# Upper two levels of a table lookup: masks on ScalarE as borders of the index, in place of bits on VectorE

## The chip, the cores and the metric

The kernel runs on one core of one Trainium2 chip. The metric is the device time of one execution in microseconds (us). Engines are named as the profile names them: PE is TensorE (matmul), PEld its weight loads, DVE is VectorE, ACT is ScalarE, POOL is GpSimd, SP is SyncE, which issues most DMAs. Each engine works through its own queue in order; an instruction that waits holds up all that stands behind it on that engine.

## The reference

Input x is 8 x 1024 x 512 (float32). What is computed, cut to what matters:

```
xn = layernorm(x)
q  = xn @ Wq ; gate = softmax(xn @ Wg)                       # 3 gates
blended = sum_i gate_i * (((q @ k_i.T) * decay_i**dist * causal) @ v_i)
s  = blended @ Wo * out_scale
w  = lut[idx]         # for gate_idx, up_idx (1376 x 512), down_idx (512 x 1376); lut has 16 floats
h  = silu(xn @ w_gate.T) * (xn @ w_up.T) ; f = h @ w_down.T
out = x + s * silu(f)
```

The change lies in `w = lut[idx]`: each index is an integer from 0 to 15, and each weight is one of 16 table values.

## The kernel before, in words

The work has two phases. Phase 1 (about the first 588 us of the profile) goes over the eight batches of x: layernorm statistics, transposes, projections to values and features, and the recurrent part chunk by chunk. Beside it, it turns the indices into float weights and writes those, with sums of their blocks, to DRAM. Phase 2 is the feed-forward part and the output: large products on PE with PSUM banks copied and added by ACT and DVE.

In phase 1 everything is written as generators that are advanced in turn; `keep_order` then fixes the order in which the code was traced, on PE, DVE, ACT and POOL. An iteration of the loop at L762 (one chunk of 128 rows, some 9.5 us) has this order:

1. `project` of the newer batch: transposes on PE (`pt` L452), copy to SBUF by ACT (`xnT` L453), normalizing and statistics by ACT (L446, L447, L436, L437), with POOL for the power (L438, L439);
2. `chunks` of the older batch: transposes `pk` (L670) on PE, three scaled copies by ACT (`ks` L673);
3. one step of the weight builder (L778), steps of the features (L520 on PE, with copies by ACT at L533 to L558 and sums by DVE at L530 to L555), one or two builder steps (L785);
4. `chunks`: scores `psc` (L677) on PE, DVE multiplies them (`pr` L679) and prepares the next queries (`ga` L652), POOL `qb` (L656);
5. three or four builder steps (L787), a step of the features;
6. `project`: values `pv` (L459) on PE, copy by ACT (`v` L462); `chunks`: `pu` (L687) and `po` (L701) on PE, copies by ACT (`bl` L702, `R` L708, `pu` L715).

The PSUM tiles pt, pk, psc, pv, po rotate through three banks (`p_c`). So the next pk takes the bank of pv, and can't start until ACT has copied v (L462); the next psc takes that of po.

The builder (`ffn_weights`) runs through 16 lookups: eleven for gate and up (128 partitions x 1024 indices, the last 768), one for the tail of down (96 x 512) and four for down (1024). A seventeenth (`left_weights`, 1024) lies in phase 2, at 603 to 666 us. They are numbered 1 to 17 here. Index tiles are loaded by SP one lookup ahead (two buffers).

A lookup (`look_up`, L215) is a binary tree. Three instructions on DVE (L220) take bits 1, 2 and 3 of the index as byte masks; one (L223) turns the index in place into a word that is all ones where bit 0 is set. Eight leaves (L227) give one of two table values each by bit 0, and seven predicated copies (L244) choose between neighbours: bit 1 at level 1, bit 2 at level 2, bit 3 at level 3. The three bits, L223, each leaf and each copy are one builder step each, 19 in all. The mask tiles have one buffer each, so a mask of one lookup can't be written until the last copy of the lookup before that reads it is done.

Of the kernel before, what the change touches and what calls it, by code (L numbers as in the profile page):

```python
# [9 lines left out]
F32 = mybir.dt.float32  # L10
BF16 = mybir.dt.bfloat16
I32 = mybir.dt.int32
U8 = mybir.dt.uint8
AF = mybir.ActivationFunctionType
ALU = mybir.AluOpType
AX = mybir.AxisListType

P = 128
# [30 lines left out]
def recurrent_block(ctx: ExitStack, tc, x, wq, wk, wv, wo, wg, decay_logits, out_scale, lut, gidx, uidx, didx, out):  # L49
# [19 lines left out]
    nc = tc.nc  # L69
# [16 lines left out]
    const = ctx.enter_context(tc.tile_pool(name="const", bufs=1))  # L86
# [62 lines left out]
    make_identity(nc, ident)  # L149
    nhalf = const.tile([P, 1], F32)  # L150
    nc.gpsimd.memset(nhalf, -0.5)


    dl = const.tile([P, NI], F32)
# [59 lines left out]

    def look_up(build, dst, iv, rows, n):  # L215

        bits = [build.tile([P, n], U8, name=f"bit{j}", tag=f"bit{j}") for j in (1, 2, 3)]
        low = iv.bitcast(U8).rearrange("p (n four) -> p n four", four=4)[:, :, 0]
        for j in (1, 2, 3):
            nc.vector.tensor_scalar(bits[j - 1][:rows, :n], low, 1 << j, None, ALU.bitwise_and)  # L220
            yield

        nc.vector.tensor_scalar(iv, iv, 31, 31, ALU.logical_shift_left, ALU.arith_shift_right)  # L223
        yield

        def leaf(o, k):
            nc.vector.tensor_scalar(  # L227
                o.bitcast(I32),
                iv,
                lut_x[:rows, k, :],  # L230
                lut_i[:rows, k, 0:1],
                ALU.bitwise_and,
                ALU.bitwise_xor,
            )

        def tree(o, level, k):
            if level == 0:
                leaf(o, k)
                yield
                return  # L240
            t = build.tile([P, n], F32, name=f"leaf{level}", tag=f"leaf{level}")
            yield from tree(o, level - 1, k)
            yield from tree(t[:rows, :n], level - 1, k + (1 << (level - 1)))
            nc.vector.copy_predicated(o, bits[level - 1][:rows, :n], t[:rows, :n])  # L244
            yield

        yield from tree(dst, 3, 0)

    def ffn_weights(build, pool, pair_pool):
# [10 lines left out]
        def gate_up(o):  # L260
# [15 lines left out]
            yield  # L276
            wf = pool.tile([P, 2 * NB], F32, name="wgu", tag="wgu", bufs=3)
            yield from look_up(build, wf[:, :n], idx[:, :n], P, n)
            if m < P:
                w = [wf[:, ts(k, 2 * m)] for k in range(4)] + [wf[:, n + k * 2 * m :][:, : 2 * m] for k in range(4)]  # L280
# [38 lines left out]
        def down_tail():  # L319
            s, m = OCH[-1]  # L320
            idx = build.tile([P, NB], I32, name="idx", tag="idx", bufs=2)
            nc.sync.dma_start(out=idx[:m, :V], in_=didx[s : s + m, :])
            yield
            wf = pool.tile([P, 2 * NB], F32, name="wgu", tag="wgu", bufs=3)
            yield from look_up(build, wf[:m, :V], idx[:m, :V], m, V)
            defer(2, lambda: nc.sync.dma_start(out=wdt_d, in_=wf[:m, :V]))

        def down(rows, e):
# [3 lines left out]
            yield  # L332
            t = pool.tile([P, 2 * NB], F32, name="wgu", tag="wgu", bufs=3)
            yield from look_up(build, t[:, : 2 * V], idx, P, 2 * V)
            b11, b12, b21, b22, t1, t2, t4 = (t[:, ts(k, V // 2)] for k in range(7))
            nc.gpsimd.tensor_tensor(t1, b12, b11, ALU.subtract)
# [1207 lines left out]
```

## Time and profile before

| | |
|---|---|
| time, median of 3 runs | 2086.72 us (2084.59 to 2086.76) |
| the profiled execution's own time | 2085.11 us, of which its span is 2083.3 us |
| PE, PEld busy | 99%, 84% of the span |
| DVE, ACT, POOL busy | 70%, 45%, 50% of the span |
| granted TensorE clock | 1.00 throughout |
| bits L220, phase 1, 128x1024 | 42 instructions, 46.1 us, mean 1138 ns |
| predicated copies L244, all | 119 instructions |
| ACT table loads | 2: at 2.9 us (1283 ns) and at the start of phase 2 |

How to read it: "idle before" is time for which the engine that issues an instruction stood still just before it, and the name behind the arrow is what ended that. "PE busy" is not PE at its best pace: what counts is whether one matmul starts as soon as the one before lets it. In the timeline a row gives its start, its duration, engine and line, what is written and read, and in brackets the idle time before it. A row that stands for several instructions ends with their number (x3).

### The profile page before, as it was taken

The page shows a single profiled execution, that of the slowest core. Times are in us where ns is not written, and L with a number is a line of the kernel's source. Part 1 is how long each engine was busy: PE and PEld are TensorE (multiplying, and loading weights), DVE is VectorE, ACT ScalarE, POOL GpSimd, SP SyncE. Part 2 cuts the span into 40 slices and gives each one's busy share as a digit, 9 for nine tenths or more (in the row PEclk, how much of TensorE's full clock was granted, in tenths as well). Part 3 has the DMA queues.
Part 4 walks back from the last instruction along what each step waited for, and adds up shares of the span by engine and source line. Part 5 has one row for each costly group of instructions (what it writes and reads, how often), then busy time and mean ns, then how long its engine had stood idle before and what let it go on. Part 6 is the DMA issues. An engine that isn't in the chain of part 4 may idle for free.

```text
span 2083.3 us, 32914 instructions
## 1 busy us (share of the span) xinstructions
PE 2068.4 (99%) x12043; PEld 1755.3 (84%) x12043; DVE 1462.5 (70%) x2246; ACT 944.1 (45%) x2133; POOL 1043.8 (50%) x1042
## 2 busy tenths in 40 slices
PE   9999999999999999999999999999999999999999
PEld 7887888788888888897888888888978888797887
DVE  8989898788458775675577557656755765675567
ACT  4767766676444424423442442344144324423531
POOL 4554665244356446516543751755275255627442
PEclk9999999999999999999999999999999999999999
DMA  9866778756764734463464447345544734464442
GB/s 231 157 176 181 188 192 178 202 126 185 168 225 154 249 142 155 168 243 133 155 228 160 154 154 261 129 160 192 198 153 153 261 129 151 170 232 144 150 162 104
DMA packets 178494, 367.23 MB, mean 176 GB/s; under 512 B 37871, under 2 KB 113278, under 8 KB 178334
## 3 DMA queue, kind: packets, MB, share of 16 engines
q1 hardware_dynamic: 161734, 338.11, 53.0%
q10 hardware_dynamic: 12120, 12.34, 1.9%
q0 software_dynamic: 4480, 14.68, 1.7%
q8 instruction: 96, 1.57, 0.3%
q14 instruction: 64, 0.52, 0.1%
HBM read 285.36 MB, written 79.73 MB: 175 GB/s over the span
## 4 chain that ended last, share of the span: by engine, by line
PE 92%; DVE 5%; DMA 2%; issue 1%; ACT 0%; SPq 0%; POOL 0%; ACTq 0%; DVEq 0%; POOLq 0%
PE s L963 34%; PE pv L459 6%; PE sE L963 6%; PE s11d L1226 5%; PE s12d L1226 5%; PE s21d L1226 5%; PE po L701 3%; PE pd L1344 3%; PE ps L1351 3%; PE sEd L1226 2%; PE pe L520 2%; PE fs L875 2%; PE pc L520 2%; PE pa L520 2%; PE psc L677 2%; PE pu L687 1%
## 5 line engine op out<-in xcount | busy, mean ns | idle before, releaser
L963 PE MATMUL s<-xs,wq 128*128 128x256 f32 x3264 | 731.6, 379 | 0.6 <-DVE s L986 0.6
L963 PEld LDWEIGHTS s<-xs,wq 128*128 128x128 f32 x3264 | 619.3, 190 | 96.8 <-issue 7.6
L986 DVE TENSOR_TENSOR s<-s,e 128x512 f32<-128x512 f32 x136 | 95.1, 699 | 188.9 <-ACT s L985 188.9
L1315 POOL TENSOR_TENSOR cu<-cu 128x256 f32<-128x256 f32 x32 | 35.1, 1097 | 328.7 <-DVE cl L1314 328.7
L459 PE MATMUL pv<-wvg_sb,xnT 128*128 128x387 f32 x512 | 177.4, 488 | 0.0
L848 POOL TENSOR_TENSOR xs<-xs 128x256 f32<-128x256 f32 x224 | 171.1, 790 | 8.5 <-PE fr L890 4.0
L990 DVE TENSOR_TENSOR sE<-s,e 128x512 f32<-128x512 f32 x136 | 95.0, 699 | 103.2 <-PE s L963 103.1
L1058 POOL TENSOR_TENSOR u<-u,e 128x512 f32<-128x512 f32 x64 | 81.7, 1299 | 147.7 <-DVE u L1054 129.2
L981 ACT COPY e<-sE 128x512 f32<-128x512 f32 x136 | 79.6, 585 | 139.6 <-PE sE L963 137.1
L963 PE MATMUL sE<-xs,wq 128*128 128x256 f32 x544 | 139.6, 379 | 0.0
L459 PEld LDWEIGHTS pv<-wvg_sb,xnT 128*128 128x128 f32 x512 | 94.2, 190 | 53.7
L1062 POOL TENSOR_TENSOR h<-h,u 128x512 f32<-128x512 f32 x64 | 81.1, 1288 | 108.1 <-DVE u L1069 108.1
L438 POOL TENSOR_SCALAR rstd<-rstd 128x1 f32<-128x1 f32 x56 | 26.1, 467 | 209.8 <-ACT junk L437 208.8
L974 ACT COPY s<-s 128x512 f32<-128x512 f32 x136 | 77.5, 570 | 110.2 <-PE s L963 105.1
L985 ACT COPY s<-s 128x512 f32<-128x512 f32 x136 | 77.5, 570 | 97.5 <-PE s L963 97.5
L1226 PE MATMUL s12d<-wdd,z 128*128 128x128 f32 x896 | 118.4, 275 | 0.6 <-ACT s12d L1248 0.6
L963 PEld LDWEIGHTS sE<-xs,wq 128*128 128x128 f32 x544 | 103.4, 190 | 14.1
L1226 PEld LDWEIGHTS s12d<-wdd,z 128*128 128x128 f32 x896 | 109.0, 192 | 0.8 <-ACT s12d L1248 0.8
L227 DVE TENSOR_SCALAR leaf<-idx,lut_x,lut_sb 128x1024 int32<-128x1024 int32 (+2 forms) x119 | 107.7, 930 | 0.0
L656 POOL TENSOR_TENSOR qb<-ga,q_tab 128x384 f32<-128x384 f32 x56 | 75.4, 1346 | 56.1 <-DVE ga L652 26.4
L244 DVE COPY_PREDICATED leaf<-bit,leaf 128x1024 f32<-128x1024 uint8 (+2 forms) x68 | 93.5, 1375 | 1.7
L1355 POOL TENSOR_TENSOR gx<-gx,cu 128x512 f32<-128x512 f32 x32 | 40.7, 1277 | 82.0 <-DVE cu L1353 64.5
(272 smaller groups left out, 4554.4 us busy)
## 6 DMA issues: line engine op xcount, KB each, us to landing
wq<-quadd SPq DMA_DIRECT2D x112, 896.0 KB, 4.5
wdd<-wdd SPq DMA_DIRECT2D x56, 896.0 KB, 5.0
xs<-xsd SPq DMA_DIRECT2D x56, 512.0 KB, 6.4
wq<-quadd SPq DMA_DIRECT2D x48, 448.0 KB, 3.8
x<-in_x SPq DMA_DIRECT2D x64, 256.0 KB, 6.3
xsd<-xnT SPq DMA_DIRECT2D x32, 512.0 KB, 10.9
xsd<-ts SPq DMA_DIRECT2D x16, 1024.0 KB, 16.1
gx<-in_x SPq DMA_DIRECT2D x64, 256.0 KB, 6.4
```

Source lines behind the costliest of these rows:

```text
L227: nc.vector.tensor_scalar(o.bitcast(I32), iv, lut_x[:rows, k, :], lut_i[:rows, k, 0:1], ALU.bitwise_and, ALU.bitwise_xor,)
L244: nc.vector.copy_predicated(o, bits[level - 1][:rows, :n], t[:rows, :n])
L459: nc.tensor.matmul(pv, lhsT=xnT[:, v, ts(c, P)], rhs=wvg_sb[:, v, :], start=(v == 0), stop=(v == NV - 1))
L520: nc.tensor.matmul(ps[:, j, :], lhsT=lhs[k][:, v, ts(j, D)], rhs=rhs[k][:, v, :], start=start and j == 0 and v == 0, stop=False, skip_grou ...
L848: nc.gpsimd.tensor_tensor(o, x1, x2, ALU.subtract)
L963: nc.tensor.matmul(self.t[n][:, ts(a, H)], lhsT=self.w[:, a, (0, 1, 6, 3, 4, 5, 2)[i - 1], :], rhs=self.xs[:, X_OF[self.ks[a]], D_OF[i], : ...
L981: nc.scalar.copy(self.e, self.t[3])
L986: nc.vector.tensor_tensor(self.t[1], self.t[1], self.e, ALU.add)
L990: nc.vector.tensor_tensor(self.t[3], self.t[2], self.e, ALU.add)
L1058: nc.gpsimd.tensor_tensor(o[:, n], o[:, n], other[:, n], ALU.add)
L1062: nc.gpsimd.tensor_tensor(of_h(half, n), of_h(half, n), two(other[:, n]), ALU.mult)
L1226: nc.tensor.matmul(self.t[n][:, ts(a, P)], lhsT=self.lhs[i][:, e, ts(a, P)], rhs=self.w[:, e, D_OF[i], :], start=start and a == 0 and e == ...
```

## The change

Bit 1 stays with DVE. The masks of levels 2 and 3 are no longer bits: ACT writes Relu(index - 3), Relu(index - 11) and Relu(index - 7) as bytes, each non-zero where the index lies above the border. Level 3 uses "above 7"; level 2 uses "above 3" in the lower half of the table (k = 0) and "above 11" in the upper (k = 4). There are so three masks by ACT where there were two bits by DVE, and four mask tiles where there were three. A constant tile of the three borders is set by POOL at the start. The number of builder steps stays 19: the first holds the bit by DVE and the first mask by ACT, the next two hold one mask each. The masks read the index tile that L223 overwrites, so L223 has to wait for the third of them.

```diff
     nc.gpsimd.memset(nhalf, -0.5)
+    below = const.tile([P, 3], F32)
+    for j, n in enumerate((3, 11, 7)):
+        nc.gpsimd.memset(below[:, j : j + 1], -float(n))
...
-        bits = [build.tile([P, n], U8, name=f"bit{j}", tag=f"bit{j}") for j in (1, 2, 3)]
+        second, *over = [build.tile([P, n], U8, name=f"bit{j}", tag=f"bit{j}") for j in range(4)]
         low = iv.bitcast(U8).rearrange("p (n four) -> p n four", four=4)[:, :, 0]
-        for j in (1, 2, 3):
-            nc.vector.tensor_scalar(bits[j - 1][:rows, :n], low, 1 << j, None, ALU.bitwise_and)
+        nc.vector.tensor_scalar(second[:rows, :n], low, 2, None, ALU.bitwise_and)
+        for j in range(3):
+            nc.scalar.activation(over[j][:rows, :n], iv, AF.Relu, bias=below[:rows, j : j + 1])
             yield
 
         nc.vector.tensor_scalar(iv, iv, 31, 31, ALU.logical_shift_left, ALU.arith_shift_right)
...
-            nc.vector.copy_predicated(o, bits[level - 1][:rows, :n], t[:rows, :n])
+            mask = second if level == 1 else over[2] if level == 3 else over[k // 4]
+            nc.vector.copy_predicated(o, mask[:rows, :n], t[:rows, :n])
             yield
```

## The prediction

> **What bounds the kernel now.** First the page's busy times:
>
> ```profile
> PE 2068.4 (99%) x12043; PEld 1755.3 (84%) x12043; DVE 1462.5 (70%) x2246; ACT 944.1 (45%) x2133; POOL 1043.8 (50%) x1042
> ```
>
> Then three windows of phase 1 (columns: window, length, then busy us of PE, PEld, DVE, ACT, POOL with counts, granted clock, DMA share, GB/s):
>
> ```profile
> 50.00:200.00 150.00, 146.41 (x831) 120.55 (x829) 139.27 (x166) 101.03 (x268) 83.79 (x76) 1.00 0.72 176
> 200.00:350.00 150.00, 149.27 (x860) 124.74 (x859) 137.52 (x167) 105.34 (x281) 90.39 (x79) 1.00 0.75 186
> 350.00:500.00 150.00, 148.54 (x858) 123.69 (x857) 120.10 (x170) 103.74 (x275) 58.17 (x64) 1.00 0.76 168
> ```
>
> The lookups lie here. DVE is the fullest engine beside PE (139.27 of 150 us), ACT has about a third free. Yet PE stands still for a few us only. Second, therefore, the waits of PE and of its weight loads in phase 1 (total us, times, longest):
>
> ```profile
> PEld pe L520 <- DVE ts L530: 4.2, 5, 2.1
> ...
> PE pe L520 <- DVE ts L530: 2.7, 3, 1.5
> ...
> PE po L701 <- DVE pr L679: 2.4, 3, 1.5
> ```
>
> Third, the timeline, matmul by matmul. Matmuls of one shape start at a constant pace (a 128x256 one each 0.216 us), and what the next start lacks against this pace is PE's loss. By it PE loses to DVE, from 50 to 240 us: 1.66 us at 98, 0.54 at 121, 0.19, 0.45 and 1.00 between 172 and 195, 0.75 at 226, sum 4.6. Later there are 0.31 at 334 and 1.62 at 377, the last behind a DMA of the gates (ga) for which DVE had waited; all are 6.5. So the most that a relieved DVE can give is 6.5 us, 0.3% of the run, and the 4.6 alone follow lookups closely.
>
> **What is taken from DVE.** Two bits a lookup. These rows have the prices (busy us, mean ns; idle before):
>
> ```profile
> L220 DVE TENSOR_SCALAR bit<-idx 128x1024 uint8<-128x1024 uint8 x42 | 46.1, 1138 | 0.8 <-DMA idx<-in_uidx 0.8
> ...
> L437 ACT ACTIVATE junk<-x,mean 128x512 bf16<-128x512 f32 x56 | 40.4, 722 | 1.8
> L453 ACT COPY xnT<-pt 128x512 f32<-128x512 f32 x64 | 37.8, 590 | 9.2 <-PE pt L452 6.9 <-DMA x<-in_x 1.9 <-DMA wdd<-pair 0.5
> L462 ACT COPY v<-pv 128x387 f32<-128x387 f32 x64 | 31.1, 486 | 59.6 <-PE pv L459 55.4 <-DMA xsd<-xnT 2.2 <-issue 1.9
> L702 ACT COPY bl<-po 128x128 f32<-128x128 f32 x64 | 17.0, 265 | 102.7 <-PE po L701 102.7
> ```
>
> Two thirds of 46.1 are 30.7 us, 33 with the smaller shapes, over 16 lookups. One bit takes 0.69 us where POOL's rows beside it are short, and up to 2.58 us where POOL sums 128x896 pairs (third and fifth lookup): there DVE stands in the way of POOL and POOL of DVE. The Trainium skill (SBUF — State Buffer, the section on its two separate sides) says that a DVE operation in a two-port mode and POOL lock each other out for a whole instruction while ACT has ports of its own; it agrees with 0.69 against 2.58, and by it a mask on ACT would not be stretched. No row here shows that for ACT writing bytes, and the sum does not use it.
>
> **What a mask costs on ACT.** The trace has no ACT instruction on 128x1024, none from int32 and none to bytes. Between 128x128 (265) and 128x512 (590) copies grow by 0.846 ns an element. The nearest form is L437 (per-partition bias, narrower output): 722 + 512 x 0.846 = 1.155 us. Lower end: a copy, 590 + 433 = 1.02. Upper end: two of the costliest 128x512 form, L447 at 814, = 1.63. I take 1.155, three in a row 3.46 us (128x768: 2.8; 96x512: 2.1), 53 us of ACT in phase 1.
>
> The ScalarE: Activation LUTs page of the Trainium skill (What ACT_TABLE_LOAD costs) puts an ACTIVATE with a pointer bias at about 280 ns + 0.833 ns an element, so an estimate of 1.13 us, which would lower the sum below by under 1 us; its rules for kernel authors speak against the change, since they give relu to VectorE as up to three times faster.
>
> **Where they stand.** The builder steps fall at L778, L785 and L787, so in ACT's queue the masks come behind ks (L673) and the features' copies, mostly all three in front of the copy of v (L462). For each lookup the order of the code tells which ACT instructions stand before and behind them. Two queues are now tied: L223 on DVE waits for the third mask, and ACT waits for the index tile and for the last copies of the lookup before. Three things follow.
>
> (a) *Late copies of v.* With no idle time ahead of it the copy comes up to 3.5 us later, and pk takes its bank. Ninth lookup:
>
> ```profile
> 279.00 0.60 ACT L544 COPY qk<-pb 128x512 f32<-128x512 f32 x1
> 279.48 0.60 ACT L549 COPY qk<-pa 128x512 f32<-128x512 f32 x1
> ...
> 280.55 0.48 ACT L462 COPY v<-pv 128x387 f32<-128x387 f32 x1 [0.47 <-PE pv L459]
> ...
> 282.27 2.45 DVE L223 TENSOR_SCALAR idx<-idx 128x1024 int32<-128x1024 int32 x1
> ...
> 282.79 0.49 PE L670 MATMUL pk<-ident,qk 128*128 128x128 f32 x3
> ```
>
> The masks come behind L544, which ends at 279.60, and end at 283.06; L549 is 3.57 late, v 3.10 (its idle 0.47 goes), so v ends at 284.13, and pk, due at 282.79, is 1.34 late. The same for the others: second lookup 0.98, third 0.92, fifth 1.96, eighth 0.82, eleventh 0.65; sum 6.7. In the first, fourth, seventh, tenth and twelfth to sixteenth ACT has idle time (1.95 to 2.37 us ahead of v) or PE comes late enough; cost 0, and without that cover about 1 us each. The sixth: 0 too.
>
> (b) *DVE waits for ACT.* Where DVE had run ahead of ACT, L223 now comes later. Sixteenth lookup:
>
> ```profile
> 502.37 0.86 ACT L673 ACTIVATE ks<-pk,k_tab 128x128 f32<-128x128 f32 x3
> ...
> 503.71 0.69 DVE L223 TENSOR_SCALAR idx<-idx 128x1024 int32<-128x1024 int32 x1
> ...
> 510.93 0.54 DVE L679 TENSOR_TENSOR pr<-psc,w_tab 128x384 f32<-128x384 f32 x1
> ...
> 513.43 0.83 PE L701 MATMUL po<-qb,R 128*128 128x128 f32 x6
> ```
>
> Masks from 503.23 to 506.69: L223 is 2.98 late, and behind it leaves, qk (L555) and pr, which comes 2.88 late and ends at 514.35; po, due at 513.43, is 0.92 late. So also the sixth (L223 0.74 late, PE 0.65), the tenth (its third mask stands behind ks of the next iteration: 2.48 late, and 2.15 at po near 334), the fourteenth (0.35), the fifteenth (1.27); in the second, ninth, eleventh, thirteenth L223 comes 0.8 to 2.9 late and DVE's next idle time takes it up. Sum 5.3.
>
> (c) *L223 earlier*, by 0.7 to 1.3 us, in the third, fourth, fifth, seventh, eighth and twelfth, where POOL had stretched the bits; the first by more, at no one's gain. This, and PE's own coming late under (a), which leaves it less to wait for, gives the 4.6 us of 50 to 240 back.
>
> Sum: 6.7 + 5.3 - 4.6 = +7.4 us. I take +7, since PE's late coming in (a) also hides some of (b).
>
> **At no cost:** the three memsets by POOL (nhalf took 0.10 us, and POOL then idles 3.55 us until the first statistics); if that cover went, 0.3 us. The seventeenth lookup, in phase 2: ACT idles 0.2 to 2.0 us ahead of its copies and DVE 0.5 to 2.4 ahead of its sums; bound without cover 3 x 0.65 = 2 us. The added semaphore waits: the ones on DVE's queue at L227 took 21 ns each in the median, some 100 of them over all queues 2 us, spread. No DMA is moved; the index loads wait for the last leaf as before.
>
> Against the profiled run's own 2085.11 us this makes 2092.1. That run is 1.6 us under the median of 2086.72, so a median of runs may read 2093.7; I give 2092.5.
>
> **Rivals.**
> - *DVE's relief decides* (faster). Place: po and pe on PE behind pr and ts, 50 to 240 us. Price: the 4.6 us, at most 6.5: 2080.5 (2078.6). For it: DVE over 90% busy, stretched bits. Against: L223 waits for the masks in eight or nine lookups. It decides if a mask takes under some 0.75 us, for then three end within the slack that (a) shows (2.2 to 2.8 us in four of its six).
> - *All is absorbed*: ACT's third of free time and the idle of DVE after 350 us take up (a) and (b), and the 4.6 are regained in part: 2083 to 2088. For it: 55 us of ACT's idle ahead of v. Against: the idle lies in iterations other than those of (a).
> - *The two queues tie each other up* (slower still): masks at 1.63 us, 4.9 a burst, 1.43 more; times six places of (a) and five of (b) 15.7 us, so 2108; at half that 2100. For it: int32 in, bytes out is an unseen form.
> - *Table loads*: were Relu in another table, two loads of 1.28 us a lookup, 41 us on ACT, would bring 2110 and more. Against: Copy, Square, Identity and Exp share one load before.
>
> **How the numbers follow.** About 0.2% (4.2 us) can be told from no change. Forecast 0.48, its own range 2089 to 2098 (mask 1.02 to 1.25, the latter 814 + 433: 11 places x -0.4 to +0.28, so -4.5 to +3; 0.05 of it within 0.2%); all absorbed 0.23; relief decides 0.10; tied queues 0.16; table loads 0.03. Faster 0.10, same 0.28, slower 0.62. The range holds the forecast, the absorbed case and the lower half of the tied one: 2083 to 2101.
>
> **What would show it.** ACT rows of 128x1024 bytes, 45 of them, at 1.1 to 1.2 us; two thirds of the L220 rows gone; idle of DVE before L223 with ACT as its end, some 40 us in all (33 of bits gone and the lateness of (b)); new waits of pk (L670) for the copy of v; waits of pe and po for DVE smaller up to 240 us, larger after 300. Wrong it would be if masks take 0.7 us or less, if PE shows no wait at pk, or if ACT waits long for DVE's last copies, which I put at under 2 us (fourth lookup alone: the copy ends at 115.81, ACT is there at 113.96).

## The result, and the profile after

The changed kernel takes 2089.75 us (median of 22 runs, 2088.64 to 2093.5) against 2086.05 us for the kernel before (22 runs, 2083.69 to 2088.4): a ratio of 1.0018, 95% interval 1.0011 to 1.0025. It is slower by 3.7 us, clearly so, and just inside the 0.2% that the prediction set as the bound of what can be told from no change, so by that bound it falls under "same" (0.28) and not under "slower" (0.62). The profiled execution took 2089.26 us, of which its span is 2087.5 us, 4.2 more than before.

Line numbers below are those of the changed kernel: five higher than before from `look_up`'s end on (L459 is now L464), the masks stand at L224, the bit at L222, the word of bit 0 at L227. The page's busy times:

```profile
PE 2070.3 (99%) x12043; PEld 1757.2 (84%) x12043; DVE 1420.6 (68%) x2212; ACT 994.2 (48%) x2184; POOL 1025.4 (49%) x1045
```

The windows of phase 1 (window, length, busy us of PE, PEld, DVE, ACT, POOL with counts, granted clock, DMA share, GB/s):

```profile
50.00:200.00 150.00, 147.08 (x838) 121.44 (x837) 120.20 (x158) 116.55 (x284) 75.71 (x77) 1.00 0.67 176
200.00:350.00 150.00, 147.16 (x836) 122.43 (x835) 124.07 (x155) 113.57 (x282) 85.01 (x78) 0.99 0.74 183
350.00:500.00 150.00, 148.91 (x852) 123.41 (x851) 110.23 (x160) 118.44 (x293) 56.58 (x66) 1.00 0.77 172
```

In the first of them DVE falls from 139.27 to 120.20 us and ACT rises from 101.03 to 116.55. DVE has been relieved as meant, but PE has gained little: seven matmul instructions more in this window (838 against 831), 24 fewer in the next (836 against 860). The groups of the masks (busy us, mean ns) and the waits in phase 1 (who waited for whom: total us, times, longest) say why:

```profile
L224 ACT ACTIVATE bit<-idx,below 128x1024 uint8<-128x1024 int32 x42 | 45.7, 1151 | 2.2 <-DMA idx<-in_uidx 2.2
...
L227 DVE TENSOR_SCALAR idx<-idx 128x1024 int32<-128x1024 int32 x14 | 13.1, 932 | 39.5 <-ACT bit L224 37.5 <-issue 2.0
```

```profile
DVE idx L227 <- ACT bit L224: 42.9, 14, 5.7
...
PEld pk L675 <- ACT v L467: 4.6, 6, 1.6
...
PE pk L675 <- ACT v L467: 3.1, 5, 1.4
...
PEld po L706 <- DVE pr L684: 2.5, 3, 2.1
...
PEld pe L525 <- DVE ts L535: 1.9, 2, 1.0
```

DVE now stands idle for 42.9 us in front of the word of bit 0, waiting for masks: more than the two bits had cost. The first line was nowhere before, nor were the waits of pk for the copy of v. The waits of pe for DVE, 4.2 us before, are 1.9.

Where the span's 4.2 us come from is read by setting the starts of the same matmuls of both traces side by side. After minus before, at matmuls of the trace of before:

| at (us, before) | after minus before | what lies ahead of it |
|---|---|---|
| 90 | +1.4 | pk waits for v: 0.50 and 0.49 |
| 100 | -0.2 | the 1.66 us wait for pr is gone |
| 118 | +0.8 | pk waits for v, fourth lookup: 0.95 |
| 122 | -0.5 | waits of 0.72 at psc and 0.54 at pe are gone |
| 155 | +1.0 | pk waits for v, fifth lookup: 1.57 |
| 195 | -0.8 | the waits for pr and ts from 172 on are gone |
| 227 | -1.4 | the 0.75 us wait is gone |
| 283 | -0.4 | pk waits: 0.37 and 0.85 |
| 335 | +1.8 | po waits 2.11 us for pr, tenth lookup; 0.31 of it was there before |
| 338 | +3.5 | TensorE at half clock for 3.4 us |
| 379 | +2.3 | a wait of 1.62 us for ts is now 0.36 |
| 482 | +3.4 | pe waits 1.01 us for ts, fifteenth lookup |
| 553 | +4.1 | a wait for ga behind a DMA, 1.37 us in place of 0.70 |
| end | +4.2 | phase 2 adds nothing |

The tenth lookup is the dearest place. Its timeline (start, duration, engine, line, what, idle before):

```profile
314.60 1.15 ACT L224 ACTIVATE bit<-idx,below 128x1024 uint8<-128x1024 int32 x1
...
315.78 0.69 DVE L227 TENSOR_SCALAR idx<-idx 128x1024 int32<-128x1024 int32 x1 [5.74 <-ACT bit L224]
...
335.80 0.55 DVE L684 TENSOR_TENSOR pr<-psc,w_tab 128x384 f32<-128x384 f32 x1
...
336.39 0.74 PEld L706 LDWEIGHTS po<-pr,v 128*128 128x128 f32 x6 [2.14 <-DVE pr L684]
```

DVE idles 5.74 us for the third mask, which stands in ACT's queue behind ks of the next iteration; it is then behind through a whole lookup without idle time, and 20 us later pr is 1.8 us late and PE stands still for 2.1.

### The profile page after: what moved, and what is told of

It is laid out like the page before. It is cut to its first block, busy times and chain, and to the rows that moved or that the text cites. A ratio compares the mean times of both kernels' runs of the same rounds, so it can differ in the third digit from the quotient of the medians.

```text
span 2087.5 us, 32942 instructions
## 1 busy us (share of the span) xinstructions
PE 2070.3 (99%) x12043; PEld 1757.2 (84%) x12043; DVE 1420.6 (68%) x2212; ACT 994.2 (48%) x2184; POOL 1025.4 (49%) x1045
## 3 DMA queue, kind: packets, MB, share of 16 engines
q8 instruction: 96, 1.57, 0.3%
## 4 chain that ended last, share of the span: by engine, by line
PE 91%; ACT 4%; DVE 2%; DMA 2%; issue 1%; POOL 0%; ACTq 0%; SPq 0%; DVEq 0%; POOLq 0%
PE s L968 34%; PE pv L464 6%; PE sE L968 6%; PE s11d L1231 5%; PE s12d L1231 5%; PE s21d L1231 5%; PE po L706 3%; PE pd L1349 3%; PE ps L1356 3%; PE sEd L1231 2%; PE pe L525 2%; PE fs L880 2%; PE pc L525 2%; PE pa L525 2%; PE psc L682 1%; PE pu L692 1%
## 5 line engine op out<-in xcount | busy, mean ns | idle before, releaser
L464 PE MATMUL pv<-wvg_sb,xnT 128*128 128x387 f32 x512 | 177.7, 489 | 0.2 <-DMA wvg_sb<-in_wv 0.2
L464 PEld LDWEIGHTS pv<-wvg_sb,xnT 128*128 128x128 f32 x512 | 94.1, 190 | 54.4 <-issue 0.4
L1067 POOL TENSOR_TENSOR h<-h,e 128x512 f32<-128x512 f32 x64 | 81.3, 1306 | 0.0
```

The costliest lines, as they stand in the source:

```text
L464: nc.tensor.matmul(pv, lhsT=xnT[:, v, ts(c, P)], rhs=wvg_sb[:, v, :], start=(v == 0), stop=(v == NV - 1))
L1067: nc.gpsimd.tensor_tensor(of_h(half, n), of_h(half, n), two(other[:, n]), ALU.mult)
```

## The experiments

Theory: three masks in a row make ACT's copy of v late, and pk with it; DVE's word of bit 0 overwrites the index that the masks read, so it waits for the third mask (this wait is called the tie below), and most of DVE's relief is lost by it; what relief is left shortens PE's waits for pr and ts. Rivals: ACT's load as such is the whole cost; or DVE's relief was worth nothing from the start.

The runs were made in two sets, each on one chip together with the kernel before, which took 2084.49 us in the first set (the relief alone, the first attempts, the masks ahead for all lookups) and 2084.51 us in the second (the others). The changed kernel was timed apart from them, against 2086.05 us; differences are always taken from the kernel before of the same set.

### The relief alone

```diff
         for j in (1, 2, 3):
-            nc.vector.tensor_scalar(bits[j - 1][:rows, :n], low, 1 << j, None, ALU.bitwise_and)
+            if j == 1:
+                nc.vector.tensor_scalar(bits[0][:rows, :n], low, 2, None, ALU.bitwise_and)
             yield
...
-            nc.vector.copy_predicated(o, bits[level - 1][:rows, :n], t[:rows, :n])
+            nc.vector.copy_predicated(o, bits[0][:rows, :n], t[:rows, :n])
```

> The kernel before with VectorE's bits 2 and 3 left out and the mask of bit 1 used at all three levels (so the weights are not those of the reference); nothing is added on ScalarE. It measures VectorE's relief alone. The theory: 4.6 to 6.5 us below the kernel before, about 2079.5 to 2081.5. Rival, that VectorE's relief is worth nothing since TensorE waits for something else: within 1 us of the kernel before.

Measured: 2078.40 us against 2084.49, ratio 0.9970 (0.9959 to 0.9981), 6.1 us less. Of PE's waits for DVE between 50 and 590 us these are left:

```profile
PEld pe L521 <- DVE ts L531: 2.5, 2, 2.1
...
PE pe L521 <- DVE ts L531: 1.7, 2, 1.5
...
PEld po L702 <- DVE pr L680: 0.2, 1, 0.2
```

So two bits of DVE are worth 6.1 us to PE, although PE counts as 99% busy and DVE as 70% over the span. The rival that the relief is worth nothing is out, and 6.1 us (4 to 8.5 by the interval) is the most that any way of moving the two bits can bring through DVE (the ceiling, below).

### The load alone, and both without the tie: a first attempt with a flaw

```diff
-    def look_up(build, dst, iv, rows, n):
+    def look_up(build, dst, iv, rows, n, odd=None):
...
-        nc.vector.tensor_scalar(iv, iv, 31, 31, ALU.logical_shift_left, ALU.arith_shift_right)
+        if odd is None:
+            odd = iv
+        nc.vector.tensor_scalar(odd, iv, 31, 31, ALU.logical_shift_left, ALU.arith_shift_right)
...
-                iv,
+                odd,
...
-            yield from look_up(build, wf[:, :n], idx[:, :n], P, n)
+            yield from look_up(build, wf[:, :n], idx[:, :n], P, n, wf[:, n : 2 * n].bitcast(I32))
```

That is the changed kernel without the tie (the calls of the down weights likewise). For the load alone the same is done to the kernel before, with the tile of the three borders, and each of the three builder steps gets a mask that nobody reads:

```diff
...
+        more = build.tile([P, n], U8, name="more", tag="more")
         for j in (1, 2, 3):
             nc.vector.tensor_scalar(bits[j - 1][:rows, :n], low, 1 << j, None, ALU.bitwise_and)
+            nc.scalar.activation(more[:rows, :n], iv, AF.Relu, bias=below[:rows, j - 1 : j])
             yield
```

> The changed kernel, but L223's word (all ones by bit 0) goes to a free part of the weight tile and not into the index, in all lookups but the seventeenth: VectorE needs no longer wait for ScalarE's third mask there. The theory (late copies of v on ScalarE, plus VectorE's wait, less VectorE's relief): without the wait VectorE keeps its relief; the 2.1 us at 334 and the 1.0 us at 484 that TensorE lost go, and the copies of v stay late by some 5 us in sum, so 1.6 us below the kernel before to 0.5 us above it, about 2084.5 to 2086.5. Rival, that ScalarE's load is the whole cost: still 3 to 4 us above the kernel before.

> The kernel before, all three bits still by VectorE, with three masks a lookup added on ScalarE that nobody reads, and L223's word put beside the index so that VectorE doesn't wait for ScalarE (in the seventeenth lookup it does). It measures the late copies of v alone. The theory: the waits of pk for v return with about 5 us, but those up to 195 us fall where TensorE would have waited for VectorE a little later anyway, so 1.5 to 3 us above the kernel before. Rival, that ScalarE's load is the whole cost: 3.7 us or more above. Rival, that it is nothing: within 0.7 us.

Measured: without the tie 2087.61 us, ratio 1.0016 (1.0007 to 1.0025), 3.1 us more than before; the load alone 2092.07 us, ratio 1.0035 (1.0022 to 1.0047), 7.6 us more. Both missed what the theory expects, and the first looks like the rival's number. The traces show a fault of the experiment. From 35.8 us on, in the first batch of x, PE loses 2.2 us (1.9 in the other) behind ACT, and in no other kernel more than 0.3 us there. On ACT's queue a DMA of the gates is issued late, first in the kernel before, then without the tie:

```profile
32.07 0.57 ACTq L491 DMA_DIRECT2D gTd<-gs  x1
```

```profile
36.04 0.57 ACTq L498 DMA_DIRECT2D gTd<-gs  x1
36.65 0.48 ACT L469 COPY v<-pv 128x387 f32<-128x387 f32 x1 [5.80 <-PE pc L527]
```

The semaphores in the traces tell why. In the kernel before, this DMA waits on the semaphore that an earlier store of `xsd` also uses (issued at 18.15, landed at 31.99 us). Without the tie it has been given another one, shared with a load of x (issued at 28.21, landed at 35.96 us), and goes out only then; the copy of v behind it, and PE, wait too. The edit had moved a semaphore, not only the tie. These two runs are therefore no test of the theory.

### The same from the third lookup on

```diff
+    done = []
...
+        done.append(dst)
-        if odd is None:
+        if odd is None or len(done) < 3:
             odd = iv
```

With this the DMA keeps its old semaphore in both kernels (issued at 33.56 and 31.64 us).

> As the run without the tie, but L223's word goes beside the index only from the third lookup on. In the run before this, a DMA of the gates on ScalarE's queue (the gs write, issued at 32 us in the kernel before) was given another semaphore, waited for a late load and went out at 36 us; TensorE lost 2.2 us there, which has nothing to do with the theory. Here that DMA has the semaphore of the kernel before. The theory: without VectorE's wait, 1 to 2.5 us below the kernel before. Rival, that the tie cost nothing and ScalarE's load is the whole cost: 3 to 4 us above, as the changed kernel.

> Three unread masks a lookup on ScalarE, all bits still by VectorE, no tie from the third lookup on, and the DMA of the gates at 32 us as before. The theory: late copies of v, partly hidden where TensorE would have waited for VectorE: 1.5 to 3.5 us above the kernel before. Rival, that ScalarE's load is the whole cost of the change: 3.7 us or more with no waits of TensorE for VectorE left.

Measured: without the tie 2082.24 us against 2084.51, ratio 0.9990 (0.9981 to 0.9998), 2.3 us less; the load alone 2086.60 us, ratio 1.0009 (1.0000 to 1.0017), 2.1 us more. Both lie where the theory expects them, and both intervals end close to no change. The waits of phase 1 without the tie:

```profile
PEld pe L530 <- DVE ts L540: 3.2, 2, 2.2
...
PEld pk L680 <- ACT v L472: 2.9, 4, 1.6
...
DVE idx L232 <- ACT bit L226: 1.7, 1, 1.7
```

DVE's wait for masks has gone from 42.9 us to 1.7 (one of the first two lookups), those of pk for v remain. So the tie alone is worth the difference between 3.7 us above and 2.3 us below: 6.0 us, give or take some 2 by the two intervals, about as much as the whole relief. The rival that ACT's load is the whole cost is out: the load has the same masks here.

The two effects do not simply add up: -6.1 and +2.1 would be -4.0, and -2.3 was measured. These medians alone do not show it, as 1.7 us lies within the intervals; the traces do. With the load alone pk is late by 5.5 us in sum, but PE's old waits for DVE are still there (0.55 us at 100, 0.53 at 122, 0.67 at 227), and a late copy of v costs nothing where PE would have waited for DVE next. Once DVE is relieved, each late copy counts in full: 0.48, 1.55, 0.34 and 0.83 us, 3.2 in the trace without the tie. Another 1.0 us of that trace has to do with neither: at 48 us PE waits for ts, since DVE had waited 1.00 us for a DMA of the gates (ga).

### Half of the change

```diff
+    below = const.tile([P, 1], F32)
+    nc.gpsimd.memset(below, -7.0)
...
         for j in (1, 2, 3):
-            nc.vector.tensor_scalar(bits[j - 1][:rows, :n], low, 1 << j, None, ALU.bitwise_and)
+            if j < 3:
+                nc.vector.tensor_scalar(bits[j - 1][:rows, :n], low, 1 << j, None, ALU.bitwise_and)
+            if j == 1:
+                nc.scalar.activation(bits[2][:rows, :n], iv, AF.Relu, bias=below[:rows, :])
             yield
```

> Half of the change: only the mask of level 3 by ScalarE (index above 7), in the first builder step; bits 1 and 2 by VectorE as before. VectorE is relieved of one bit a lookup (some 17 us instead of 33), ScalarE has one mask of 1.15 us in place of three in a row. The theory: a copy of v is late by 1.15 us at most, within the slack nearly everywhere, L223 waits little, since two bits on VectorE take longer than one mask; half of the relief is left: 2 to 4 us below the kernel before. Rival, that any mask on ScalarE costs what it saves: within 1 us.

Measured: 2082.46 us against 2084.51, ratio 0.9990 (0.9981 to 0.9999), 2.05 us less, the lower end of what was expected. The waits of phase 1:

```profile
DVE idx L228 <- ACT bit L225: 5.3, 6, 1.2
...
ACT bit L225 <- DVE wgu L249: 3.4, 3, 1.9
```

No pk waits for v for more than 0.2 us. The tie is still there and costs 5.3 us of DVE in place of 42.9. A third of the ceiling is reached by moving one bit instead of two, with one mask in place of three; the change as made moved more and lost.

### The masks one lookup ahead

The masks of the next lookup go, one at a time, behind the sixth, tenth and fourteenth leaf or copy of the lookup at hand, into the half of the next weight tile that its sums fill only later.

```diff
+    AHEAD = (6, 10, 14)
+    def masks_of(room, iv, rows, n):
+        def of(j):
+            t = room[:rows, n : 2 * n].bitcast(U8)[:, j * n : (j + 1) * n]
+            nc.scalar.activation(t, iv, AF.Relu, bias=below[:rows, j : j + 1])
+            made.append(t)
+        made = []
+        coming.append((made, of))
...
+        over, of = coming.pop(0)
+        while len(over) < 3:
+            of(len(over))
...
+        def one_ahead():
+            nonlocal steps
+            steps += 1
+            if steps in AHEAD and coming and len(coming[0][0]) < 3:
+                coming[0][1](len(coming[0][0]))
```

It was run twice: for all lookups of phase 1, where the DMA of the gates was late again (34.75 us), and from the third lookup on, where it was not.

> The changed kernel with the masks made one lookup ahead, one at a time, at the sixth, tenth and fourteenth leaf or copy of the lookup before, in the still free half of the next weight tile. ScalarE has the same 48 masks in phase 1, but never three in a row, and VectorE finds them done. The theory: a copy of v is late by 1.15 us at most, under the slack of most places, VectorE waits for no mask, and its relief remains: 4 to 6 us below the kernel before, about 2080 to 2082. Rival, that ScalarE's load as such costs: at the kernel before or above.

> The masks made one lookup ahead, one at a time, from the third lookup on (the first two as in the changed kernel), with the DMA of the gates at 32 us as before. The theory: VectorE's relief stays nearly whole, 5 to 7 us below the kernel before, about as the run with the relief alone. Rival, that the first two lookups' tie and the spread masks cost: 2 to 4 us below.

Measured: 2079.70 us, ratio 0.9980 (0.9971 to 0.9989), and 2079.64 us, ratio 0.9977 (0.9967 to 0.9987): 4.8 and 4.9 us less than before, some 8.5 us less than the changed kernel, and the fastest complete kernel here. The second lies at the edge between its two expectations. Its windows:

```profile
50.00:200.00 150.00, 149.14 (x859) 124.15 (x858) 131.72 (x164) 120.37 (x293) 77.10 (x76) 1.00 0.67 177
200.00:350.00 150.00, 150.00 (x866) 125.32 (x865) 127.25 (x154) 118.22 (x294) 92.30 (x81) 1.00 0.78 189
```

ACT is as full as in the changed kernel (120.37 against 116.55 us in the first window), and PE does 859 matmul instructions in it where that does 838. So it isn't the work on ACT that costs, but three masks at one place and a wait behind them. What is still missing to the ceiling are one wait of 3.4 us of DVE in the second lookup, and waits of pk of 0.51 and 0.67 us in the second and fourth; two masks still stand next to each other on ACT at seven places, where two builder steps lie close.

## Why the prediction was right, and where its sizes were off

It forecast slower by 7 us (2092.5, range 2083 to 2101); measured were 3.7 us. Direction and mechanism held; the size was forecast at about twice what it came to. That the range held says little, since it reached from 3 us below the kernel before to 15 above it.

- *What DVE can give.* Predicted 4.6 us, at most 6.5. The relief alone gave 6.1. Right.
- *A mask.* Predicted 1.155 us, measured 1151 ns in the mean of 42. Right; int32 in and bytes out cost nothing extra, and no table was loaded on the way. But "three in a row 3.46 us" was too long: the trace has 3.23, since each starts some 0.11 us before the one ahead has ended. The prediction's own rows already had this: L544 starts at 279.00 and takes 0.60, and L549 starts at 279.48. The ScalarE: Activation LUTs page of the Trainium skill (What ACT_TABLE_LOAD costs) states such an overlap of about 93 ns; the prediction cited this place for the time of one and left the overlap out. The ninth lookup in the changed kernel:

```profile
278.27 3.24 ACT L224 ACTIVATE bit<-idx,below 128x1024 uint8<-128x1024 int32 x3
281.40 0.59 ACT L554 COPY qk<-pa 128x512 f32<-128x512 f32 x1
```

- *(a) Late copies of v.* Predicted 6.7 us at six places. Measured 4.9 at seven: 0.50, 0.49, 1.57, 0.37, 0.85 and 0.21 at the six named (for 0.98, 0.92, 1.96, 0.82, 1.34 and 0.65), about 0.45 less each. That is four overlaps of 0.11: two within the burst, one with the copy ahead of it and one with the copy behind it. To these come 0.95 in the fourth, which was put at nothing. There ACT came to the masks at 115.22 and not at 113.96, as its copies ahead of them were late themselves. The term was mis-sized by the length of the burst, and by taking ACT's place in time from the old trace.
- *(b) The tie.* Predicted 5.3 us at five places. The two large ones came nearly as worked out: 2.11 us (2.15) in the tenth, of which 0.31 had been there before, and 1.01 (1.27) in the fifteenth. The three small ones (0.65, 0.35, 0.92) did not. The burst that is 0.45 shorter takes up the 0.35 and most of the 0.65. The 0.92 of the sixteenth was also counted from the wrong row: the matmuls of po at 513.43 read qb and R, and those that read pr start at 514.10 (row below), so that pr at 514.35 would have been 0.25 late. DVE's idle before the word of bit 0, put at some 40 us, is 42.9. By the runs the tie as a whole is worth 6.0 us, since it also takes away relief that would have come without it; as a difference of two kernels that is a larger thing than PE's waits that can be pointed at. The row of the kernel before:

```profile
514.10 0.83 PE L701 MATMUL po<-pr,v 128*128 128x128 f32 x6
```

- *(c) The relief that is left.* Predicted 4.6 us back between 50 and 240 us; 4.5 of it came. The list lacked another 0.72 us, at the psc of 120.89 us in the trace of before. The profile puts that wait to ACT's L446, but it goes with the relief alone as well and stays with the load alone, so it belongs to DVE, whose ga ends at 120.79. The wait at 377 us, which was left out as lying behind a DMA, shrank too, by 1.26 us.
- *Not in the sum:* 1.7 us of half clock in the profiled execution, 0.7 us more behind the DMA of the gates at 553, and 0.3 us ahead of 50 us. The half clock is not shown to be part of the 3.7 us: a fall of 3.41 us takes 0.0008 off a run's mean clock, and the ten of the 22 runs with a mean of 1.000 took 2089.68 us in the median, the other twelve 2089.77.

With the measured steps the sum is 4.9 + 2.8 - 5.2 - 1.3 + 1.7 + 0.7 + 0.3 = 3.9 us, against 4.2 in the spans; the rest lies in steps of 0.1 and 0.2. The terms that were mis-sized are (a), 6.7 for 4.9, and (b), 5.3 for 2.8, mostly by the four overlaps at each burst, and (c), 4.6 for 6.5 with the wait at 377 us. By these three terms alone the trace has 1.2 us where the prediction has 7.4. That the result lies nearer owes something to luck, as the half clock, the DMA and the start, 2.7 us of the profiled execution, were in no term.

The rival "DVE's relief decides" had its point at a mask under 0.75 us. The way around turned out to be another: the same mask of 1.15 us, at another place, gives 80% of the relief. That the price hung on the place and not on the length was in the working (its slacks of 2.2 to 2.8 us, in four of the six places of (a), exceed one mask), but no rival was made of it.

## What to carry to other kernels

When work is moved to an engine with free time, count two things besides its busy share: what stands behind it in that engine's queue, and who must now wait for it. Here an in-place overwrite on the old engine turned a reader on the new one into a wait of 43 us, and three instructions in a row hurt where the same three apart did not. Issue moved work early and spread, into a buffer that nobody overwrites, and leave out the tie before judging the move.

When an experiment edits buffers, look first whether anything else moved: here a DMA's completion semaphore did. PE lost some 2 us by it in the two profiles, the medians differ by 5.4 and 5.5 us from those of the runs in which it kept its place (the two sets ran on different chips), and the effect that was to be measured was hidden.

## What the runs showed of the hardware that was not expected

TensorE's clock fell to half after a wait of some 2 us. In the changed kernel's profile PE's weight loads stand idle for 2.14 us up to 336.39, its matmuls for 1.95; these windows follow (columns as above, the clock is the third last):

```profile
334.00:338.00 4.00, 2.05 (x16) 1.86 (x15) 3.96 (x5) 0.57 (x2) 1.94 (x3) 0.92 1.08 393
338.00:341.00 3.00, 3.00 (x11) 2.50 (x10) 1.94 (x4) 2.88 (x7) 2.92 (x3) 0.54 0.54 202
341.00:345.00 4.00, 4.00 (x21) 3.24 (x20) 2.76 (x4) 2.14 (x8) 3.75 (x4) 1.00 0.77 266
```

The clock's own record has 0.5 for 3.41 us from 337.4, and PE loses another 1.7 us, nearly as much as by the wait. The page TensorE: Matmul & The Clock Gate of the Trainium skill (Part 1: The HAM clock gate) has the clock fall after an idle window of about 3.4 us. The length of 3.41 us fits such a window; that it takes a whole idle one does not, as here 2.1 us of idle time were enough.

It does not always come, and where the wait lies seems to count. All stretches of full clock in the records are multiples of 3.413 us (331.09 us ahead of this fall are 97 of them, the 2075.30 us of the kernel before 608). Counted on this grid, the step from 333.96 to 337.38 us, right ahead of the fall, holds 1.95 us without a matmul. The first kernel without the tie has a wait as long (no matmul for 2.00 us from 36.17 on), but a border of its grid at 37.75 parts it into 1.58 and 0.42 us, and there is no fall. Of all other steps in the ten traces, from the start of full clock to the end of PE's work, none holds more than 1.74 us, and none is followed by a fall. With one fall amid the work on record this is a reading and not yet a rule.

That profiled execution of the first kernel without the tie took 2084.66 us at a mean clock of 1.000, while its other ten runs have mean clocks of 0.998 or 0.999 and take 2086.07 to 2090.61 us. That those runs lose the clock at this wait was not seen, only that they run at the lower mean.
